# Which queue issues the first loads of a fused attention, gate and expert block, and when the biases are loaded

## The chip, the core and the metric

The kernel runs on one core of a Trainium2 chip. Its time is device microseconds of one execution. The kernel before takes 307.41 us, the median of 3 runs (307.2 to 307.61).

## The reference

The input x has 1,024 tokens (2 batches of 512) of 1,024 columns. Per batch there is a context of 1,024 rows and 1,024 columns. Cut to what matters:

```python
def fake_quant(x, scale, zp):
    q = jnp.clip(jnp.round(x / scale + zp), 0, 255)
    return (q - zp) * scale

# the "attention": a quantized product, gated by a scalar
x = x + tanh(g_xattn) * fake_quant(layernorm(x)) @ fake_quant(ctx)
# a shared MLP and two routed experts of 16, gated by a scalar
xt = layernorm(x)
z = silu(xt @ sw1 + sb1) * (xt @ sw2 + sb2) @ sw3 + sb3
y = sum over chosen experts of gate * (silu(xt @ ew1 + eb1) * (xt @ ew2 + eb2) @ ew3 + eb3)
x = x + tanh(g_ffn) * (y + z)
```

The change touches only how the first inputs come into the core. Nothing that is computed changes.

## The kernel before, in words

The tokens are eight tiles of 128 (tiles 0 to 3 are batch 0, tiles 4 to 7 batch 1). A first stage, which ends some 60 us into the run, does for each tile: statistics of the two halves (`bn`, L182, and `ag`, L186, on VectorE), the reciprocal root (`qp`, L195, on GpSimd), scale and offset (`qr`, L199 and L200), the quantized tile (`q8`, L214), the centred bf16 copy `qx` (`qc`), eight transposes on TensorE (`qt`, L225) and their copy `qT` (`qe`, L163). The context comes in eight row tiles per batch, each quantized to bytes (`c8`, L238 or L240) and centred to bf16 in `cq` (`cc`, L167 or L169). TensorE then multiplies qT by cq (`mm`, L250), and VectorE adds the product to x (`e`, L262). What follows, the second layer norm, the shared MLP, the routing, the experts and the down products, keeps TensorE at work to the end.

The order of the first stage is written out by hand. `START` (L43) is a list of steps with the engine that runs each, and the instructions of every engine stand in the order of that list; an engine does not pass an instruction that waits. `kb` steps are matmuls of zeros (L554) that fill TensorE's time. Step `pb` (L559) transposes the biases on TensorE, and `bt` (L562) copies them to where later activations take them from.

The loads are issued ahead of that list. In program order they are: the scalars `sc_in` (L118: the quantization's scales and zero points and the two gates, broadcast to 128 partitions, 3 KB); tile 0 of x in two column halves of 256 KB, by `load_x(0, 2)` (L514, which calls L133); then the list `LOADS` (L42). There `x.t` is a tile of x (512 KB, L133), `c.k` a row tile of the first context (512 KB, L508; `c.7` in two halves), `b` the biases of all hidden layers (72 rows of 512 B, L525), and `w.c.i` a weight slice of the shared MLP (512 KB in rows of 512 B, L498; in the profile sa0r, sb1r, sa1r and sb0r). Step `ld` (L594), further on in START, issues the second context and tiles 6 and 7 of x. All of these loads are issued by SyncE, so its queue alone sets their order.

Each load signals its end on a semaphore. There are eight, taken in turn, so a load that takes one again waits, on the queue that issues it, until the load eight before it has landed. By 8.9 us SyncE is at the tenth of these loads and waits in that way.

On the other engines the stage starts as follows. ScalarE loads its function table, runs a warm-up activation on a constant (L139), and takes the tanh of the gates (L528), for which it needs the scalars. VectorE sets constants, takes reciprocal, negation and a few more small results of the scalars (L145 to L153, L530, L531), and begins the statistics of tile 0. TensorE runs fillers.

Of the kernel before, what the change touches and what calls it, by code (L numbers as in the profile page):

```python
# [18 lines left out]
P = 128  # L19
# [19 lines left out]
LOWEST = -3.4028234663852886e38  # L39


LOADS = "x.1 x.3 c.0 c.1 c.2 b c.4 c.3 x.2 c.5 x.4 c.6 c.7.0 c.7.1 x.5 w.0.0 w.1.1 w.1.0 w.0.1"  # L42
START = """  # L43
bn.0.0 bn.0.1 ag.0 qa.0.dve xx.0 qp.0 kb.12 kb.1 qr.0.dve kb.3 q8.0.dve.0 qc.0.act.0 stage.0 kb.7 qt.0.0 bn.1.0 bn.1.1
bn.3.0 ag.1 bn.3.1 ag.3 qa.1.pool c8.0.0.act.0 qp.1 q8.0.dve.1 qa.3.dve qc.0.dve.1 cc.0.0.act.0 kb.2 qr.1.pool
# [32 lines left out]
def flamingo_block(  # L78
# [3 lines left out]
    nc = tc.nc  # L82
    xf = x.rearrange("b s d -> (b s) d")
# [14 lines left out]
    def slab(name, dtype, shape=(P, D)):  # L98
        return slabs.tile(list(shape), dtype, tag="slab", name=name)
# [15 lines left out]


    sc_in = const.tile([P, 6], F32, name="sc_in")
    nc.sync.dma_start(sc_in, scal.partition_broadcast(P))  # L118


    X = [None] * NT
# [5 lines left out]
    dq = [nc.sync]  # L127

    def load_x(t, parts=1):
        X[t] = slab(f"X{t}", F32)  # L130
        for h in range(parts):
            cols = ts(h, D // parts)
            dq[0].dma_start(X[t][:, cols], xf[ts(t, P), cols])  # L133


    mhalf = const.tile([P, 1], F32, name="mhalf")
# [36 lines left out]
    cols = lambda h: slice(None) if h is None else half(h)  # L173
# [337 lines left out]
    wr = {}  # L511
    NB = 2 * SC + 2 * E * EC
    br = const.tile([NB, P], F32, name="br")
    load_x(0, 2)  # L514
    for load in LOADS.split():
        kind, *at = load.split(".")
        at = [int(a) for a in at]
        if kind == "x":
            load_x(*at)
        elif kind == "c":  # L520
            load_c(0, *at)
        elif kind == "w":
            load_w(*at)
        else:
            nc.sync.dma_start(br, hbias)  # L525
# [68 lines left out]
    def ld():  # L594
        for k in range(KD):
            load_c(1, k)
        load_x(6)
        load_x(7)
# [410 lines left out]
    for n in range(SC, NC):  # L1009
        j, c = divmod(n - SC, EC)  # L1010
# [223 lines left out]
```

## Time and profile before

| | |
|---|---|
| median of 3 runs | 307.41 us |
| the profiled execution: its own time | 308.87 us |
| its span, first to last instruction | 307.1 us |
| granted TensorE clock | 0.998 |
| busy: TensorE, its weight loads | 296.7, 232.0 us |
| busy: VectorE, ScalarE, GpSimd | 216.9, 150.3, 88.0 us |
| HBM read, written | 39.76, 12.59 MB |
| chain that ended last: TensorE, DMA, SyncE's queue | 81%, 11%, 3% |

The page cuts the span in 40 slices of 7.7 us and gives a digit for the busy tenths of each. SPq is the queue of SyncE: the time in which it issues DMAs or waits to. A row of the timeline has start, duration, engine, line, operation, what it writes and reads, a count, and in brackets how long the engine stood idle before it and what ended that. A row of the stage table has the stretch, its length, busy time and count of the five engines, the granted clock, the busy share of the DMA engines and what they moved in GB/s. In the first 45 us the core reads 14.85 MB, 330 GB/s on average, nearly all of it in the queue of the hardware DMAs that SyncE issues.

### The profile page before, as it was taken

The page shows a single profiled execution, that of the slowest core. Times are in us where ns is not written, and L with a number is a line of the kernel's source. Part 1 is how long each engine was busy: PE and PEld are TensorE (multiplying, and loading weights), DVE is VectorE, ACT ScalarE, POOL GpSimd, SP SyncE. Part 2 cuts the span into 40 slices and gives each one's busy share as a digit, 9 for nine tenths or more (in the row PEclk, how much of TensorE's full clock was granted, in tenths as well). Part 3 has the DMA queues.
Part 4 walks back from the last instruction along what each step waited for, and adds up shares of the span by engine and source line. Part 5 has one row for each costly group of instructions (what it writes and reads, how often), then busy time and mean ns, then how long its engine had stood idle before and what let it go on. Part 6 is the DMA issues. An engine that isn't in the chain of part 4 may idle for free.

```text
span 307.1 us, 4234 instructions
## 1 busy us (share of the span) xinstructions
PE 296.7 (97%) x1500; PEld 232.0 (76%) x1500; DVE 216.9 (71%) x370; ACT 150.3 (49%) x213; POOL 88.0 (29%) x118
## 2 busy tenths in 40 slices
PE   8789998999999999999999999999999999999993
PEld 3344794599958888888888888888888888888883
DVE  4899988996848599864572658825489698657522
ACT  2689888777362374443251544417573548420000
POOL 2577796568422311400011110112420060000000
PEclk9999999999999999999999999999999999999999
DMA  6999960792159982540504208049999999812122
GB/s 187 413 405 310 384 235 1 237 393 89 37 148 197 216 158 41 109 170 32 174 2 116 90 2 239 34 128 356 299 334 324 339 220 298 271 74 100 77 99 75
DMA packets 39695, 56.91 MB, mean 185 GB/s; under 512 B 5531, under 2 KB 22755, under 8 KB 39666
## 3 DMA queue, kind: packets, MB, share of 16 engines
q1 hardware_dynamic: 36338, 48.16, 45.6%
q0 software_dynamic: 3328, 8.39, 14.5%
q8 instruction: 14, 0.23, 0.3%
q14 instruction: 15, 0.12, 0.1%
HBM read 39.76 MB, written 12.59 MB: 170 GB/s over the span
## 4 chain that ended last, share of the span: by engine, by line
PE 81%; DMA 11%; SPq 3%; DVE 1%; POOL 1%; issue 0%; POOLq 0%
PE pb L962 11%; DMA X<-in_dram 9%; PE sp L362 7%; PE pa L962 7%; PE pc L962 6%; PE sp L582 4%; PE b7B L406 3%; PE b6B L406 3%; PE b5B L406 3%; PE b4B L406 3%; PE b3B L406 3%; PE b2B L406 3%; PE at L250 3%; SPq L498 2%; DMA cr<-in_dram 2%; PE b7C L406 2%
## 5 line engine op out<-in xcount | busy, mean ns | idle before, releaser
L250 PE MATMUL at<-cq,qT 128*128 128x512 bf16 x128 | 29.8, 379 | 1.5 <-POOL cq L169 1.0
L250 PEld LDWEIGHTS <-qT 128*128 128x128 bf16 x128 | 12.1, 97 | 15.3 <-issue 1.9
L973 DVE SCALAR_TENSOR_TENSOR Y<-pb,tg,Y 128x512 f32<-128x512 f32 x12 | 9.0, 748 | 8.3 <-PE pb L962 8.3
L809 POOL DMA_DIRECT2D xf<-xf x8 | 7.2, 938 | 22.9 <-DMA xf<-xf 13.1
L933 POOL DMA_DIRECT2D rS<-hrouted x6 | 7.3, 1600 | 22.3 <-DMA rS<-hshared 15.2
L554 PE MATMUL pz<-zero 128*128 128x512 bf16 x43 | 12.0, 436 | 1.4 <-DVE zero L547 1.4
L973 DVE SCALAR_TENSOR_TENSOR Y<-pc,tg,Y 128x512 f32<-128x512 f32 x8 | 5.9, 749 | 10.0 <-PE pc L962 10.0
L438 POOL TENSOR_TENSOR b4s<-b4s,gates 128x512 f32<-128x512 f32 x2 | 2.6, 1279 | 34.7 <-ACT b4s L448 27.9
L262 DVE SCALAR_TENSOR_TENSOR X<-at,cx_scale,X 128x512 f32<-128x512 f32 x16 | 11.7, 745 | 0.5 <-PE at L250 0.5
L238 ACT ACTIVATE q8c<-cr,sc_in,rs 128x1024 uint8<-128x1024 f32 (+1 forms) x9 | 10.2, 1135 | 3.6 <-DMA cr<-in_dram 3.6
L182 DVE BATCH_NORM_STATS2 st<-X 128x6 f32<-128x512 f32 x16 | 10.5, 677 | 1.8 <-DMA X<-in_dram 1.8
L271 ACT ACTIVATE xn<-X,s 128x512 f32<-128x512 f32 x16 | 11.5, 718 | 0.1
L315 DVE TENSOR_TENSOR XL<-px,XH 128x512 fp32r<-128x512 f32 x16 | 10.3, 679 | 0.5 <-ACT xf L322 0.5
L167 ACT ACTIVATE cq<-q8c,nz 128x1024 bf16<-128x1024 uint8 (+1 forms) x10 | 10.4, 1056 | 0.3 <-DVE q8c L240 0.2
L554 PEld LDWEIGHTS <-zero 128*128 128x128 bf16 x43 | 4.5, 110 | 7.2 <-issue 2.7
L582 PE MATMUL sp<-XH,sb 128*128 128x256 f32 x64 | 9.6, 290 | 0.3 <-ACT XH L161 0.3
L161 ACT CAST XH<-px 128x512 fp32r<-128x512 f32 x13 | 7.2, 606 | 5.0 <-PE px L305 5.0
L656 POOL TENSOR_TENSOR xf<-XH,XL 128x1024 f32<-128x1024 f32 x4 | 9.5, 2399 | 0.0
L956 DVE TENSOR_TENSOR rB<-rB,rB 128x1024 f32<-128x1024 f32 x8 | 9.2, 1217 | 0.0
L582 PEld LDWEIGHTS sp<-XH,sb 128*128 128x128 f32 x64 | 8.2, 190 | 1.1 <-ACT XH L161 0.7
L305 PE MATMUL px<-ident,xn 128*128 128x128 f32 x64 | 8.8, 274 | 0.1
L582 PE MATMUL sp<-XH,sa 128*128 128x256 f32 x64 | 8.8, 285 | 0.0
(598 smaller groups left out, 886.5 us busy)
## 6 DMA issues: line engine op xcount, KB each, us to landing
cr<-in_dram SPq DMA_DIRECT2D x15, 512.0 KB, 8.7
x_after<-X SPq DMA_DIRECT2D x8, 512.0 KB, 6.7
xf<-xf POOLq DMA_DIRECT2D x8, 512.0 KB, 5.2
rB<-in_dram SPq DMA_DIRECT2D x8, 512.0 KB, 8.9
Y<-x_after SPq DMA_DIRECT2D x8, 512.0 KB, 8.8
out_dram<-Y SPq DMA_DIRECT2D x15, 256.0 KB, 2.2
X<-in_dram SPq DMA_DIRECT2D x7, 512.0 KB, 10.1
rS<-hrouted POOLq DMA_DIRECT2D x6, 512.0 KB, 11.6
```

The source lines that it names most:

```text
L167: nc.scalar.activation(out, q8, AF.Identity, bias=nz)
L182: nc.vector.bn_stats(st_[t][:, h, :], X[t][:, half(h)])
L250: nc.tensor.matmul(acc[t][h], qT[b][:, t % TB, k, :], cq[b][k // KH][:, k % KH, half(h)], start=(k == 0), stop=(k == KD - 1))
L262: nc.vector.scalar_tensor_tensor(xs, acc[t][h], cx_scale, xs, ALU.mult, ALU.add, accum_out=sq_[t][0][:, h : h + 1])
L271: nc.scalar.activation(xn_[t][:, half(h)], X[t][:, half(h)], AF.Square, bias=s[:, h : h + 1], scale=-float(H), accum_out=q[:, h : h + 1],)
L315: nc.vector.tensor_tensor(XL[b][q][p], px_[t, q], XH[b][q][p].bitcast(F32), ALU.subtract)
L362: nc.tensor.matmul(p, wx[:, k, :], xx[b][k // KH][:, k % KH, cols], start=first and k == 0, stop=last and k == KD - 1,)
L406: nc.tensor.matmul(p, w[:, k, :], x[:, k, :], start=f and k == 0, stop=l and k == KH - 1, skip_group_check=not first,)
L554: nc.tensor.matmul(pz[0], zero[:, :P], zero, start=True, stop=True)
L582: nc.tensor.matmul(up_[c, lo, i], w[:, k, :], x[0][k // KH][:, k % KH, lo : lo + 256], start=p == 0 and k == 0, stop=p == 2 and k == KD - 1,)
L962: nc.tensor.matmul(p, x[:, ts(t, P)], w[:, cl], start=first and k == 0 and i == 0, stop=k == KH - 1 and i == 2, skip_group_check=not first,)
L973: nc.vector.scalar_tensor_tensor(X[t][:, cl], p, tgf, X[t][:, cl], ALU.mult, ALU.add)
```

## The change: who issues the first loads

Four things are done. The scalars' load goes from SyncE's queue to ScalarE's. So does the second half of tile 0; the first half stays with SyncE, and is now its first DMA. `load_x(0, 2)` is moved up, ahead of the constants and ScalarE's table load, so that both of ScalarE's DMAs stand in front of that load in its order. And `b` moves in `LOADS` from behind `c.2` to behind `x.5`, ahead of the weight slices.

```diff
-LOADS = "x.1 x.3 c.0 c.1 c.2 b c.4 c.3 x.2 c.5 x.4 c.6 c.7.0 c.7.1 x.5 w.0.0 w.1.1 w.1.0 w.0.1"
+LOADS = "x.1 x.3 c.0 c.1 c.2 c.4 c.3 x.2 c.5 x.4 c.6 c.7.0 c.7.1 x.5 b w.0.0 w.1.1 w.1.0 w.0.1"
...
     sc_in = const.tile([P, 6], F32, name="sc_in")
-    nc.sync.dma_start(sc_in, scal.partition_broadcast(P))
+    nc.scalar.dma_start(sc_in, scal.partition_broadcast(P))
...
         for h in range(parts):
             cols = ts(h, D // parts)
-            dq[0].dma_start(X[t][:, cols], xf[ts(t, P), cols])
+            (dq[0] if h == 0 else nc.scalar).dma_start(X[t][:, cols], xf[ts(t, P), cols])
+
+
+    load_x(0, 2)
...
     br = const.tile([NB, P], F32, name="br")
-    load_x(0, 2)
     for load in LOADS.split():
```

`load_x` with one part, as all other tiles of x are loaded, issues on SyncE as before. The eight semaphores are taken in program order whoever issues, so the scalars and the two halves still take the first three. With `b` gone from its place, the loads from c.4 to x.5 each take the semaphore before the one they took; the four weight slices and all that follow take the same ones as before. On VectorE the first statistics of tile 0 move ahead of three small operations on the scalars; TensorE's and GpSimd's orders stay as they are.

## The prediction, made blind

> **What bounds the kernel now.** I read the page first (busy shares, slices, its chain), then the same chain in order of time, then a table of busy time by stage, and last the timeline of the first 54 us. In the page's slices TensorE looks full from end to end, so the question is where it is not:
>
> ```profile
> PE   8789998999999999999999999999999999999993
> DMA  6999960792159982540504208049999999812122
> ```
>
> The stage table (us of the stage, then busy us and count per engine) says it in numbers:
>
> ```profile
> 0.00:18.00 18.00, 13.96 (x65) 5.85 (x65) 12.18 (x33) 8.64 (x12) 7.94 (x18) 1.00 0.87 318
> 18.00:44.00 26.00, 25.53 (x172) 17.48 (x171) 25.31 (x57) 23.09 (x34) 20.23 (x30) 1.00 1.00 350
> 44.00:54.00 10.00, 9.21 (x64) 5.16 (x63) 7.99 (x20) 8.86 (x13) 7.43 (x13) 1.00 0.01 3
> 54.00:302.00 248.00, 248.00 (x1204) 203.48 (x1202) 170.88 (x262) 109.68 (x158) 52.37 (x58) 1.00 0.58 169
> ```
>
> From 54 to 302 TensorE has no gap; behind it lie 5.1 us of last add and store. So the time is 302.0 + 5.1, and a change can only move the point at which the unbroken part begins. TensorE idles 4.04 us before 18 (more in truth: 43 of its matmuls there, L554, are fillers on zeros), 0.47 us from 18 to 44, and 0.79 us from 44 to 54. The chain in order of time (start, us, what) shows what ends each:
>
> ```profile
> 0.87 0.39 SPq L118
> ...
> 2.25 6.61 DMA X<-in_dram
> ...
> 8.88 8.99 DMA X<-in_dram
> ...
> 17.88 3.18 SPq L498
> ...
> 33.36 11.48 DMA X<-in_dram
> ```
>
> Every link until 44.84 is a load or its issue: the DMA engines are about full (share 0.87, then 1.00), and tile 7 of x lands at 44.84 as the last big load. Two places tie TensorE to this stream, and the timeline has both:
>
> ```profile
> 3.69 0.18 DVE L145 RECIPROCAL rs<-sc_in 128x4 f32<-128x4 f32 x1 [2.38 <-DMA sc_in<-in_dram]
> 5.37 0.69 DVE L182 BATCH_NORM_STATS2 st<-X 128x6 f32<-128x512 f32 x1 [0.37 <-DMA X<-in_dram]
> 8.89 1.93 DVE L182 BATCH_NORM_STATS2 st<-X 128x6 f32<-128x512 f32 x3 [0.65 <-DMA X<-in_dram]
> 11.02 0.23 POOL L191 TENSOR_SCALAR r<-mv 128x1 f32<-128x1 f32 x1 [3.87 <-DVE mv L186]
> 16.92 0.81 PE L250 MATMUL at<-cq,qT 128*128 128x512 bf16 x3 [1.01 <-POOL cq L169]
> 24.27 0.23 PE L559 MATMUL pbt<-ident,br 72*128 72x72 f32 x1
> ```
>
> Place one: VectorE stands 0.65 us until tile 1 lands at 8.86; from its statistics GpSimd works without a pause (11.02 to 16.8) up to the piece of cq that TensorE awaits at 16.92. Place two: VectorE stands 0.78 us until 44.87 for tile 7, and the qT, sa and qx behind it on VectorE cost TensorE gaps of 0.17, 0.30 and 0.32 us before 53.37: the 0.79 us. So two paths lead to 53.4: TensorE's own, set at 16.9, which is 0.8 us ahead, and tile 7's, which decides.
>
> **The change, part by part.** *SyncE's queue.* Today it issues the scalars (0.87, 0.39 us), tile 0's halves (1.31 and 1.77, 0.42 and 0.43 us) and then tile 1, at 2.25. Afterwards the first half starts at 0.87 (0.44 earlier), and tile 1 at 0.87+0.42+0.05 = 1.34: 0.91 us earlier, as are tile 3 and the first context tiles. The biases' issue (0.75 us at 5.09) no longer stands ahead of c.4; that is worth nothing more, as the loads from 8.88 on wait for landings, not for SyncE.
>
> *What the stream gains.* From 8 us on it runs at 410 to 430 GB/s, so what matters is how much earlier it gets going. Below: 0.44 us, the shift of the first byte, if tile 1 is tied to the end of tile 0 as today. Above: 0.91, the shift of tile 1's issue. I take 0.7, about the middle, since tile 1 stands right behind the first half now but shares the engines with the second. One rule of the Trainium skill bears on this: DMA: Bandwidth & Descriptors, "Issuing engines are not separate DMA queues", says that all issuers' transfers interleave on the same 16 engines, and that a second issuer only saves the sequencer's time. By it the second ring moves no byte sooner; the sum stays with these issue times (0.44 to 0.91), and I book nothing for two rings. The rows leave some room: between 4 and 5 us, with four loads issued, the engines moved only 152 GB/s, so something other than bytes held them, and a second ring might fill that (a rival below).
>
> *Tile 0 and the scalars.* ScalarE issues the scalars at 0.88 and the half at about 1.3, instead of SyncE at 0.87 and 1.77. The scalars' landing at 3.69 frees VectorE; I keep it (between -0.1 and +0.5, since they now start side by side with the first half). In the changed program VectorE takes the first statistics three small operations earlier (at about 4.0 instead of 4.31). The second half was awaited to 5.37; issued 0.46 earlier but beside tile 1, I take 5.1, between 4.9 and 5.8. VectorE's work on tile 0, which ends at 8.24, then ends near 8.0, and 0.65 us of waiting for tile 1 covers it up to 8.9. Cost nothing, gain nothing beyond tile 1's.
>
> *ScalarE.* Two issues of about 0.43 us (SyncE's rows; ScalarE has none) push its table load (row at 0.88, 1.28 us) from 0.88 to about 1.75, so the load and the 0.20 us warm-up end at 3.25, under the 3.69 at which it waits for the scalars today. Cover left: 0.4 us; if an issue took 0.2 us more on ScalarE than on SyncE it would be used up. Here a rule speaks against the change: ScalarE: Activation LUTs, "What ACT_TABLE_LOAD costs", gives a table switch 2.66 us with its drain. From 1.75 that ends at 4.41, the tanh of the gates would come 0.9 us late, and VectorE, whose cx_scale waits for it, would delay the second statistics to some 5.2. The row shows no drain (warm-up starts at 2.17, 0.01 us after the load's end), so I book zero; by the rule it would be 0.1, again inside tile 1's wait.
>
> *The biases.* Their load moves behind x.5, whose landing is 8.7 us after its issue at 15.43, so at 24.1. No row shows a small load there: between 0 and 0.5 us after x.5, I take 0.2, as 36 KB at 415 GB/s are 0.09. TensorE's transpose of them (L559) stands in order at 24.27 and now would start at 23.6 with the stream 0.7 earlier; the biases land near 23.6. A wait of 0.1 us, at most 0.5. Queued behind it are the matmuls of tiles 0, 1 and 3 and all else on TensorE. It lies on TensorE's own path, which has the 0.8 us, so it costs nothing; without that cover it would cost itself.
>
> *The semaphores.* Each load reuses the semaphore of the load eight before, and waits for its landing. Without the biases in between, c.4 to x.5 wait for one landing earlier. The weight loads, with the biases now before them, wait for one landing later: w.0.0 for x.2 (17.87) instead of c.3 (16.66), w.1.1 for the load behind it, 1.2 us later. Their issue would be late by 1.2 minus 0.7 = 0.5 us. But w.1.1 spends 3.18 us in its issue now (17.88 to 21.06) and the same sort of load 1.45 us at 24.18: 1.7 us of it is waiting for room behind the loads ahead, and covers the 0.5. Booked at zero.
>
> **Sum.** Tile 1, tile 3 and with them GpSimd's chain and TensorE's 16.92 come 0.7 us earlier, tile 7 too (44.84 to 44.1), so 53.37 becomes 52.7: the profiled execution's 308.87 (span 307.1 and 1.77 around it) becomes 308.2. It stands 1.46 above the median of the timed runs, 307.41; I take the same 0.7 off that: 306.7, which is 0.23% less. About 0.2%, or 0.6 us, is what a measurement can tell from no change.
>
> **The rivals.**
> *The engines were the limit from the start* (tile 1 lands at 8.86 whoever issues it, as its last packets wait for their turn or for the memory). For it: tile 1 needs 6.61 us from issue to landing where a half of tile 0 needs 3.0. Against it: the 152 GB/s between 4 and 5. Gain 0 to 0.3, so 307.2. Chance 0.24.
> *Two rings fill the early hole.* The dip between 4 and 5 us (152 against the 303 GB/s of the next microsecond) is worth 0.5 us; with the 0.7 the stream comes 1.2 earlier. Tile 0's own path (about 8.0, against 8.86) then limits place one to 0.9, but TensorE's path has 0.8 in hand. 306.2. Chance 0.15.
> *The weights come too late* (the slower side). If w.0.0 and w.1.1, issued one landing later, leave the rings empty near 24 us, the whole rest of the stream slips: 1.2 us at most, against 0.7 gained, so tile 7 lands 0.5 later and the time is 307.9. It decides once the issue's slack is under 0.5 us. For it: the chain runs through those very issues (3.18, 3.04, 1.45 us). Against it: the 1.7 us of waiting for room. Chance 0.16.
> *The change does not do what it says:* the order of SyncE's queue is what the diff says, only whether ScalarE's first issue is as quick is open; that is in the first rival.
>
> **How the numbers follow.** My case has 0.45, its own range 306.4 to 307.0, and two thirds of it below 306.8. Faster by over 0.2%: 0.30 + 0.15 = 0.45. Within: 0.15 + 0.22 = 0.37. Slower: 0.18, the weights with a little of the first rival. Range: 305.9 (the second rival with 0.3 to spare) to 307.9 (half of the weights' case).
>
> **What would show it.** Tile 1's statistics on VectorE at 8.2 instead of 8.89, TensorE's matmul at 16.2, tile 7's statistics at 44.2, the last gap before 52.7, all with TensorE unbroken after. ScalarE's tanh still at 3.7. The wait at L559 under 0.5. I am wrong if tile 1 stays at 8.9, if the scalars land after 4.3, or if tile 7 comes later while tile 1 came earlier (then the weights did it).

## The result: 0.7% slower, and the profile after

| | before | after |
|---|---|---|
| median of 22 timed runs each | 308.09 us | 310.08 us |
| ratio of after to before, 95% | | 1.0069 [1.0049, 1.0089] |
| the profiled execution, its span | 308.87, 307.1 us | 310.04, 308.3 us |
| VectorE takes up the scalars, just landed | 3.69 us | 4.47 us |
| VectorE takes up the second half of tile 0, just landed | 5.37 us | 7.12 us |
| statistics of tile 1 start (VectorE) | 8.89 us | 9.91 us |
| start of TensorE's unbroken part | 53.37 us | 54.53 us |

The prediction said 306.7 us, 305.9 to 307.9. The two profiles lie 1.2 us apart, and all of it has come by 54.5 us: the start of the unbroken part moved by 54.53 - 53.37 = 1.16. The kernel before varies over its 22 runs from 306.88 to 311.06; so the parts are read from the profiles, and the whole from ratios.

The stage table of the changed kernel, in the stretches and columns of the one before:

```profile
0.00:18.00 18.00, 14.17 (x60) 5.98 (x61) 10.57 (x31) 7.57 (x11) 7.01 (x18) 0.91 0.88 331
18.00:44.00 26.00, 24.94 (x161) 15.95 (x160) 25.71 (x56) 22.41 (x32) 21.48 (x31) 1.00 0.95 341
44.00:54.00 10.00, 10.00 (x69) 6.54 (x68) 8.77 (x20) 9.59 (x14) 6.78 (x12) 1.00 0.01 2
54.00:302.00 248.00, 247.76 (x1210) 203.23 (x1208) 172.23 (x265) 110.48 (x158) 53.65 (x60) 1.00 0.58 168
```

In the first row VectorE did 10.57 us of work where it did 12.18: it is behind by 18 us. The DMA engines moved more in that row (331 GB/s against 318), so the loads as a whole are not late. In the third row TensorE has no gap left: the wait for tile 7, one of my two places, is gone, and the time is longer all the same. The granted clock is 0.91 in the first row, which is new; runs below ask whether that is the cause.

The start of the chain that ended last, in order of time (start, us, what):

```profile
1.31 5.79 DMA X<-in_dram
11.20 4.26 PE pz L556 x12
```

Before, the chain's first long load was tile 1, issued at 2.25. Now it is the second half of tile 0, issued by ScalarE at 1.31 and landed 5.79 us later, for 256 KB; and no later load is among these longest pieces. The timeline shows what waits for it (lines are 2 or 3 higher than before: L185 is the statistics, L228 the transposes, L556 the fillers, L561 the biases):

```profile
0.87 1.34 SPq L133 DMA_DIRECT2D X<-in_dram  x3
0.88 0.41 ACTq L118 DMA_DIRECT2D sc_in<-in_dram  x1
...
1.31 0.45 ACTq L133 DMA_DIRECT2D X<-in_dram  x1
...
1.80 1.28 ACT L142 ACT_TABLE_LOAD   x1 [1.80 <-PEq L1222]
...
4.47 0.18 DVE L148 RECIPROCAL rs<-sc_in 128x4 f32<-128x4 f32 x1 [3.17 <-DMA sc_in<-in_dram]
...
7.12 0.33 SPq L133 DMA_DIRECT2D X<-in_dram  x1
7.12 0.69 DVE L185 BATCH_NORM_STATS2 st<-X 128x6 f32<-128x512 f32 x1 [1.55 <-DMA X<-in_dram]
7.49 0.43 SPq L511 DMA_DIRECT2D cr<-in_dram  x1
...
8.34 0.33 SPq L133 DMA_DIRECT2D X<-in_dram  x1
...
9.91 1.87 DVE L185 BATCH_NORM_STATS2 st<-X 128x6 f32<-128x512 f32 x3
...
10.80 0.40 PE L228 MATMUL pq<-ident_b,qx 128*128 128x128 bf16 x4 [2.46 <-ACT qx L170]
...
11.04 4.42 PE L556 MATMUL pz<-zero 128*128 128x512 bf16 x12
```

The scalars land 0.8 us later than before. VectorE then stands 1.55 us until the second half is there (0.37 before), and from 7.12 it works through tile 0's small steps up to 9.91, where the row of tile 1's statistics has no bracket: VectorE did not wait for tile 1. SyncE's own rows say when tile 1 and tile 3 came. Each issue there waits for the load eight before: by that the issue at 7.12 waits for the second half, the one at 7.49 for tile 1, the one at 8.34 for tile 3. (Before, the issue at 8.88, which waited for tile 1, is the twelfth load, counted from the scalars.) So tile 1 was there by 7.49 (8.86 before) and tile 3 by 8.34 (10.12 before, by the same reckoning). The trace's own landing records put tile 1 at 6.92, ahead of the second half. The loads after tile 0 came earlier, as the change suggests, and the start of tile 1's statistics gained nothing from it, because tile 0 itself came later.

How much earlier is the stream in bytes? From stage tables of one microsecond each (GB/s):

| us | 1-2 | 2-3 | 3-4 | 4-5 | 5-6 | 6-7 | 7-8 | sum to 8, MB |
|---|---|---|---|---|---|---|---|---|
| before | 0 | 127 | 334 | 152 | 303 | 250 | 401 | 1.567 |
| after | 16 | 211 | 132 | 317 | 283 | 379 | 426 | 1.764 |

0.197 MB at the 414 GB/s that follow before are 0.5 us. Yet tile 1 came 1.9 us earlier (6.92 against 8.86) and tile 3 1.8. The rest did not come from more bytes but from a changed order: SyncE's loads overtook the second half.

### The profile page after: what moved, and what is told of

Its sections match the earlier page's. It is cut to its first block, busy times and chain, and to the rows that moved or that the text cites. A ratio compares the mean times of both kernels' runs of the same rounds, so it can differ in the third digit from the quotient of the medians.

```text
span 308.3 us, 4234 instructions
## 1 busy us (share of the span) xinstructions
PE 298.0 (97%) x1500; PEld 232.7 (75%) x1500; DVE 217.9 (71%) x370; ACT 150.1 (49%) x213; POOL 88.9 (29%) x118
## 4 chain that ended last, share of the span: by engine, by line
PE 83%; DVE 9%; POOL 3%; DMA 2%; issue 1%; ACT 0%; ACTq 0%; POOLq 0%
PE pb L964 11%; PE sp L365 7%; PE pa L964 7%; PE pc L964 6%; PE sp L584 4%; PE b7B L409 3%; PE b6B L409 3%; PE b5B L409 3%; PE b4B L409 3%; PE b3B L409 3%; PE b2B L409 3%; PE at L253 3%; DMA X<-in_dram 2%; PE pz L556 2%; DVE st L185 2%; PE b7C L409 2%
## 5 line engine op out<-in xcount | busy, mean ns | idle before, releaser
L556 PE MATMUL pz<-zero 128*128 128x512 bf16 x43 | 13.5, 476 | 1.4 <-DVE zero L549 1.4
L185 DVE BATCH_NORM_STATS2 st<-X 128x6 f32<-128x512 f32 x16 | 10.3, 672 | 1.6 <-DMA X<-in_dram 1.6
L556 PEld LDWEIGHTS <-zero 128*128 128x128 bf16 x43 | 4.8, 115 | 8.1 <-issue 4.1
L170 ACT ACTIVATE qx<-q8x,nz 128x1024 bf16<-128x1024 uint8 (+1 forms) x5 | 5.3, 1061 | 8.1 <-DVE q8x L217 5.9
```

Source lines behind the costliest of these rows:

```text
L170: nc.scalar.activation(out, q8, AF.Identity, bias=nz)
L185: nc.vector.bn_stats(st_[t][:, h, :], X[t][:, half(h)])
L556: nc.tensor.matmul(pz[0], zero[:, :P], zero, start=True, stop=True)
```

## Experiments

Each of ten kernels was timed together with the kernel before on the same chip, and a ratio compares these two. The table has what decides; "start" is that of tile 1's statistics, and the landings are those of the trace's records.

| run | scalars, first, second half landed | start | span | ratio to before, 95% |
|---|---|---|---|---|
| before | 3.7, 4.3, 5.4 | 8.89 | 307.1 | |
| after | 4.5, 4.3, 7.1 | 9.91 | 308.3 | 1.0069 [1.0049, 1.0089] |
| e1_half_first | 7.6, 4.1, 4.3 | 10.73 | 309.1 | 1.0110 [1.0053, 1.0167] |
| e2_half_only | 5.5, 6.4, 5.8 | 9.82 | 308.2 | 1.0031 [1.0014, 1.0048] |
| e3_scalars_only | 4.5, 4.3, 5.9 | 8.75 | 307.1 | 0.9994 [0.9971, 1.0016] |
| e4_biases_only | 3.7, 4.3, 5.2 | 8.98 | 305.6 | 0.9982 [0.9957, 1.0006] |
| e5_more_fillers | as after | 9.95 | 308.3 | 1.0083 [1.0056, 1.0110] |
| e6_fewer_fillers | 3.9, 4.6, 5.7 | 8.49 | 306.5 | 1.0014 [0.9993, 1.0035] |
| e7_scalars_biases | 4.5, 4.3, 5.9 | 8.68 | 307.2 | 1.0004 [0.9981, 1.0027] |
| e8_scalars_gpsimd | 8.0, 4.1, 4.3 | 11.82 | 310.6 | 1.0134 [1.0103, 1.0166] |
| e9_hold_sync | 4.1, 3.9, 4.5 | 8.14 | 306.8 | 1.0012 [0.9985, 1.0038] |
| e10_changed_again | 4.3, 4.1, 7.1 | 9.93 | 308.5 | 1.0042 [1.0016, 1.0069] |

In eleven of the twelve profiles the span less the start is 298.0 to 298.8 us (before 307.1 - 8.89 = 298.2, after 298.4), while the start itself runs from 8.14 to 11.82. Only e4_biases_only is off it, with 296.6. So in these profiles the span follows tile 1's statistics nearly one for one, and the first question is what sets their start. (Why the rest is so constant is asked under e7; it is in part luck.) A start varies by some tenths by itself: e6 issues the same loads as the kernel before, and starts at 8.49 where that starts at 8.89.

### The parts, one at a time

**e1_half_first**: the changed kernel, with the two loads of ScalarE in the other order.

```diff
-    nc.scalar.dma_start(sc_in, scal.partition_broadcast(P))
...
     load_x(0, 2)
+    nc.scalar.dma_start(sc_in, scal.partition_broadcast(P))
```

> The changed kernel with ScalarE's two loads in the other order: the half of tile 0 first, then the scalars. Theory A (order within one ring: the 128 pieces of 24 B of the scalars hold ScalarE's ring until about 4.0 us, and only then does the half move, landing at 7.10): the half now lands at 4.3 to 5.3 us, the scalars at 5 to 6.5 us; statistics of tile 0 end by about 6.5, TensorE idles under 1.5 us before its first transposes instead of 2.46, and the time falls 1 to 2 us below the changed kernel's, to within 1 us of the kernel before. Theory B (sharing: the half must take turns with the deep queue of SyncE, whichever place it has): the half still lands near 6.5 to 7, the scalars later still, and the time is that of the changed kernel or more.

The half landed early as theory A had it, but the time got worse: the scalars took the half's place. The timeline:

```profile
4.11 0.69 DVE L185 BATCH_NORM_STATS2 st<-X 128x6 f32<-128x512 f32 x1 [2.81 <-DMA X<-in_dram]
...
7.66 0.18 DVE L148 RECIPROCAL rs<-sc_in 128x4 f32<-128x4 f32 x1 [2.86 <-DMA sc_in<-in_dram]
```

3 KB issued at 1.31 landed at 7.64. So it is not the size: whichever load stands second in ScalarE's ring (its queue of DMAs) is late. The view of the DMA queues from 0 to 9 us of this run (busy tenths and GB/s in 40 slices of 0.225 us) shows what the scalars do while they pass:

```profile
DMA  0000000087699999997765343253436799999999
GB/s 0 0 0 0 0 0 0 0 100 173 237 319 364 373 382 465 446 401 256 238 183 128 128 129 92 74 147 92 128 128 219 274 437 382 455 401 473 401 382 455
...
q10 hardware_dynamic: 288, 0.27, 8.3%
```

q10 is ScalarE's ring: 128 pieces of 24 B for the scalars, 128 of 2,048 B for the half, and 32 of 4 B. From 4.5 to 6.8 us, with SyncE's loads waiting in their own ring, the engines moved only 74 to 183 GB/s. The changed kernel has its dip (132 GB/s) from 3 to 4 us, where its scalars pass; before has it (152) from 4 to 5, just after they do, so the pieces explain the dip only in part.

**e2_half_only**: the kernel before, with the second half alone on ScalarE, and `load_x(0, 2)` at its new place behind the scalars' load, which stays SyncE's first.

```diff
-            dq[0].dma_start(X[t][:, cols], xf[ts(t, P), cols])
+            (dq[0] if h == 0 else nc.scalar).dma_start(X[t][:, cols], xf[ts(t, P), cols])
...
+    load_x(0, 2)
...
-    load_x(0, 2)
```

> The kernel before with one part of the change: the second half of tile 0 issued by ScalarE; scalars first on SyncE and the biases in their old place. Theory A (the scalars ahead of the half in its ring did the harm): the half lands near 4.5 to 5.3 us (5.37 before), time within 0.7 us of the kernel before. Theory B (taking turns with SyncE's loads): the half lands at 6.3 to 7.1, TensorE idles 1.5 us or more before its first transposes, and the time is 1 to 2 us over the kernel before.

Theory A fell here in its simple form: the half, alone in its ring, landed at 5.8, between the ranges of the two theories and no earlier than in the kernel before, and now the scalars (5.5) and the first half (6.4) were late in SyncE's ring.

```profile
5.52 0.18 DVE L148 RECIPROCAL rs<-sc_in 128x4 f32<-128x4 f32 x1 [4.22 <-DMA sc_in<-in_dram]
...
6.44 1.28 DVE L185 BATCH_NORM_STATS2 st<-X 128x6 f32<-128x512 f32 x2 [0.22 <-DMA X<-in_dram]
```

Two rings delay each other's first loads. SyncE's big loads are not needed for that: by the packet records, from 2.2 to 3.8 us no data passes here but about 90 pieces of the scalars and 47 packets of the half, and the engines moved 24 GB/s from 2 to 3 us and 108 from 3 to 4. So the scalars' small pieces slow what shares with them, too. In one ring, the order is a priority: before, tile 0's three loads are all in by 5.37.

**e3_scalars_only** (the kernel before with `nc.scalar.dma_start(sc_in, ...)` as the only edit) and **e7_scalars_biases** (the same and the new `LOADS`, which is the changed kernel with only the half's move undone):

> The kernel before with one part of the change: the scalars issued by ScalarE, both halves first on SyncE. Theory A: the half is safe in SyncE's ring (lands about 4.5 to 5.0), only the scalars come late (4.2 to 4.5 us against 3.69), which is inside the wait for tile 1; no 2 us idle of TensorE, loads from tile 1 on 0.4 us earlier, time 0 to 0.8 us under the kernel before. Rival C (the scalars' late landing alone delays all of tile 0): tile 0's statistics end 0.8 us later than before and the time is 0.5 to 1 us over it.

> The changed kernel with one part undone: both halves of tile 0 are on SyncE again, first in its queue; scalars on ScalarE and the biases late, as in the change. Ring theory (what stands second in ScalarE's ring comes late, since by then the deep queue of SyncE shares the engines with it): the half lands at about 5.9 as in the run with the scalars alone, no loss of clock, time within 0.5 us of the kernel before. Rival (scalars and late biases carry part of the loss): 0.6 us or more over the kernel before.

Both are within 0.3% of the kernel before. The scalars come 0.8 us late in both and the second half at 5.9, but with the halves on one ring VectorE starts tile 1's statistics at 8.75 and 8.68, a little ahead of before. So most of the loss needs the half's move: e7 and the changed kernel differ in that and in the place of `load_x(0, 2)` in the program, and the ratios are 1.0004 against 1.0042 and 1.0069.

e7 also shows where the forecast gain went. Tile 1's statistics start 0.21 us earlier than before, and VectorE's wait of 0.78 us for tile 7 is gone, yet tile 7's statistics start at 44.8 as before (44.87). Between the two, single instructions of VectorE take longer. The first case, before and then in e7:

```profile
18.55 0.75 DVE L169 TENSOR_SCALAR cq<-q8c,nz 128x1024 bf16<-128x1024 uint8 x1
...
19.27 1.19 POOL L240 TENSOR_SCALAR q8c<-cr,rs,sc_in 128x1024 uint8<-128x1024 f32 x1 [1.30 <-PE pq L225]
```

```profile
17.70 1.62 POOL L240 TENSOR_SCALAR q8c<-cr,rs,sc_in 128x1024 uint8<-128x1024 f32 x1
...
18.29 1.57 DVE L169 TENSOR_SCALAR cq<-q8c,nz 128x1024 bf16<-128x1024 uint8 x1
```

GpSimd no longer waits before it quantizes this piece of the context, so it runs beside VectorE's instruction, and both take longer (1.62 for 1.19, 1.57 for 0.75). From 31 us on it happens again: four steps of the layer norm (L300) take 2.72 us in place of 1.92, with GpSimd's next quantization beside them, which before stood 1.44 us for its load. Some later instructions are shorter in e7 and give part of it back. The long 1.57 stands in all seven profiles in which GpSimd has begun its step and not ended it (the changed kernel, e1, e2, e3, e5, e7, e10), and 0.75 in the other five; no run tests it by itself. So the earlier stream did take away the wait for tile 7, about 0.8 us, and VectorE lost about as much beside GpSimd. That the span less the start is nearly the same before and after rests on these two being of one size. e6, e8 and e9 have neither and still lie at 298.0 to 298.8; why is not shown.

**e4_biases_only** (the kernel before with the new `LOADS` list):

> The kernel before with one part of the change: the biases' load behind x.5. Theories A and B both give no more than 0.3 us either way. Rival D (the biases arrive late for TensorE's transpose, and the weight slices wait for one landing more): a wait of 0.1 to 0.5 us at that transpose, weights issued 1.2 us later than before, and a time 0.5 to 1.5 us over the kernel before.

No loss: 0.9982, and the interval [0.9957, 1.0006] includes no change. TensorE waited 0.18 us for the biases here (before it loads them as weights, L559, at 24.21). Its profile is the one off the rule, 1.6 us better than its start would give. It has neither cost: no wait for tile 7, and the two steps of VectorE at their short 0.75 and 1.92 us, so TensorE's unbroken part begins at 51.91 in place of 53.37. Why its later loads came as they did is open, and the timed runs do not show a gain of that size.

### Is it the clock?

After the 2.46 us of idling at 10.80, the next 12 fillers took 4.42 us in place of 2.75, and the granted clock of the stage is 0.91. **e5_more_fillers** gives the changed kernel eight more fillers in front of the first transposes; **e6_fewer_fillers** takes eight from the kernel before (the second pair of lines).

```diff
-bn.0.0 bn.0.1 ag.0 qa.0.dve xx.0 qp.0 kb.12 kb.1 qr.0.dve kb.3 q8.0.dve.0 qc.0.act.0 stage.0 kb.7 qt.0.0 bn.1.0 bn.1.1
+bn.0.0 bn.0.1 ag.0 qa.0.dve xx.0 qp.0 kb.20 kb.1 qr.0.dve kb.3 q8.0.dve.0 qc.0.act.0 stage.0 kb.7 qt.0.0 bn.1.0 bn.1.1
...
-bn.0.0 bn.0.1 ag.0 qa.0.dve xx.0 qp.0 kb.12 kb.1 qr.0.dve kb.3 q8.0.dve.0 qc.0.act.0 stage.0 kb.7 qt.0.0 bn.1.0 bn.1.1
+bn.0.0 bn.0.1 ag.0 qa.0.dve xx.0 qp.0 kb.4 kb.1 qr.0.dve kb.3 q8.0.dve.0 qc.0.act.0 stage.0 kb.7 qt.0.0 bn.1.0 bn.1.1
```

> The changed kernel with eight more zero matmuls ahead of tile 0's first transposes (31 instead of 23), so that TensorE does not stand the 2.46 us after which its twelve next fillers took 4.42 instead of 2.75 us (granted clock 0.91 in the first 18 us). Clock theory (TensorE's lost clock makes the kernel slow): the twelve take 2.75 us again, granted clock back near 1.00, and the time falls 1.0 to 1.7 us. Chain theory (tile 0's late half pushes VectorE, and GpSimd behind it, 1.0 us back, and TensorE's first products wait for GpSimd anyway): the fillers are quick again, but the piece of cq comes as before, and the time falls 0 to 0.3 us.

> The kernel before with eight zero matmuls fewer ahead of tile 0's first transposes (15 instead of 23), its loads untouched: TensorE now stands about 3 us before 9.05. Clock theory: its clock falls as in the changed kernel, the next twelve fillers take about 4.4 us, and the time rises 0.8 to 1.7 us with all data on time. Chain theory: the fillers are slow too, but 1.0 us of TensorE's wait for cq at 16.9 takes most of it up, and the time rises 0.2 to 0.7 us.

The timeline has the fillers after the first transposes; first of e5:

```profile
11.08 2.75 PE L556 MATMUL pz<-zero 128*128 128x512 bf16 x12
```

and of e6:

```profile
9.39 0.61 PE L225 MATMUL pq<-ident_b,qx 128*128 128x128 bf16 x4 [2.53 <-ACT qx L167]
9.79 4.07 PE L554 MATMUL pz<-zero 128*128 128x512 bf16 x12
```

e5 has its full clock back (1.00 from 0 to 18 us) and its span is the changed kernel's, 308.3. e6 lost the clock (0.91) and shows no loss that can be told from none (1.0014 [0.9993, 1.0035]). **e10_changed_again** settles it. It is the changed kernel once more, on the chip of e9:

> The changed kernel itself, on the chip of the run with SyncE held back, so that the two stand side by side. All theories: the half lands at 7.1 us, tile 1's statistics start at 9.9, 0.4 to 0.9% over the kernel before.

In that execution TensorE idled 2.30 us, the next 12 fillers took 2.75 us, the clock did not fall (1.00 from 0 to 18 us), and the span is 308.5, no better than with the fall:

```profile
7.14 0.69 DVE L185 BATCH_NORM_STATS2 st<-X 128x6 f32<-128x512 f32 x1 [1.71 <-DMA X<-in_dram]
...
9.93 1.87 DVE L185 BATCH_NORM_STATS2 st<-X 128x6 f32<-128x512 f32 x3
...
10.82 0.40 PE L228 MATMUL pq<-ident_b,qx 128*128 128x128 bf16 x4 [2.30 <-ACT qx L170]
```

The clock is an effect of the late tile, not the cause of the time.

### What holds the second load of ScalarE's ring

**e8_scalars_gpsimd**: the changed kernel with the scalars on GpSimd's queue, so that the half is alone in ScalarE's. If the half is late because it stands behind the scalars, it should come early, and the scalars as well.

```diff
-    nc.scalar.dma_start(sc_in, scal.partition_broadcast(P))
+    nc.gpsimd.dma_start(sc_in, scal.partition_broadcast(P))
```

> The changed kernel with the scalars issued by GpSimd's queue, so that the second half of tile 0 stands first in ScalarE's ring and the first half first in SyncE's. Ring theory: both halves land at 4.0 to 4.4 us (as in the run with the half first in ScalarE's ring), tile 0's statistics end by 5.9 instead of 8.1 if the scalars land by 4.5, tile 1 lands near 7, TensorE keeps its clock, and the time is 1 to 2.5 us under the changed kernel's and 0 to 1.3 us under the kernel before. Sharing theory (a third ring slows all three): scalars or a half land at 5.5 or later, and the time is no better than the kernel before.

The half did (4.3), the scalars did not: 8.0, later than in any other run, and the time is the worst of all, 1.0134.

```profile
8.02 0.18 DVE L148 RECIPROCAL rs<-sc_in 128x4 f32<-128x4 f32 x1 [6.71 <-DMA sc_in<-in_dram]
```

A queue of its own did not protect the scalars. But GpSimd's queue is of another kind (the profile lists it as software_dynamic, the other two as hardware_dynamic): the scalars went there as 16 packets of 192 B, the first at 4.73 us, 2.5 us after their issue was over. So this run does not say that sharing made them late. For the half it says more: as the first of its ring it is early beside the same stream of SyncE, here (4.3) as in e1 (4.3); its packets are through by 3.9 us, most of them while SyncE's ring is still at the first half. As the second it meets tile 1 and what follows. **e9_hold_sync** removes these loads for as long as tile 0 is under way. SyncE first stores one element of the second half to a scratch word, for which it has to wait until the half has landed, and issues tile 1 only then.

```diff
+    seen = spill.tile([1, 1], F32, name="seen")
+    with tc.manual_schedule():
+        nc.sync.dma_start(seen, X[0][0:1, D - 1 : D])
+        for load in LOADS.split():
...
```

> The changed kernel with SyncE held back: after the first half of tile 0 it issues a store of one element of the second half to a scratch word (4 bytes, read by nothing; this is the added work), for which it waits until that half has landed, and only then tile 1 and the rest. So ScalarE's two loads share the engines with the first half alone. Sharing theory (the half lands at 7.1 because tile 1 and the contexts, issued by SyncE from 1.3 us on, take turns with it): the half now lands at 4.8 to 5.6 us, tile 0's statistics end near 6.3 instead of 8.06, tile 1 is issued at about 5.2 and lands at 8.3 to 9.3, TensorE keeps its clock, and the time is 0.7 to 2 us under the changed kernel's, near that of the kernel before. Rival (a second load in ScalarE's ring is slow by itself): the half lands at 6.5 or later, tile 1 some 3 us behind it, and the time is 1 us or more over the changed kernel's.

```profile
1.31 0.45 ACTq L133 DMA_DIRECT2D X<-in_dram  x1
...
4.11 0.18 DVE L148 RECIPROCAL rs<-sc_in 128x4 f32<-128x4 f32 x1 [2.81 <-DMA sc_in<-in_dram]
...
4.51 0.30 SPq L519 DMA_DIRECT2D seen<-X  x1
...
4.86 0.84 SPq L133 DMA_DIRECT2D X<-in_dram  x2
...
5.13 0.68 DVE L185 BATCH_NORM_STATS2 st<-X 128x6 f32<-128x512 f32 x1
...
8.14 2.00 DVE L185 BATCH_NORM_STATS2 st<-X 128x6 f32<-128x512 f32 x3
```

Same issue at 1.31, same place behind the scalars in the same ring: it lands at 4.50 in place of 7.12, and the scalars at 4.1. On the same chip the median is 308.83 us, against 310.21 for e10_changed_again and 308.58 for the kernel before. With tile 1 issued 3.5 us later than in the changed kernel, 1.4 us of loss is gone. That is the cause of the half's lateness, shown from both sides: it comes with the sharing (e10) and goes with it (e9), with ring, order and issue times of tile 0's three loads kept. The time goes with it; e9 holds the whole stream back as well, so its time alone does not say how much is the half's, but e7, where only the half's move is undone, comes to the same (1.0004).

The trace's packet records fit it. In the changed kernel ScalarE's ring moves the 24 B pieces of the scalars from 2.1 to 3.9 us, and the half's 128 packets of 2,048 B only from 4.2 to 6.6, in turns with 129 packets of 4,096 B from SyncE's ring, which had been given six loads by then. In e9 the pieces pass from 2.2 to 3.6 and the half's packets from 2.8 to 4.1. So of the 2.6 us about 1.4 are a later start behind the scalars, and the rest the turns.

No version that ran clearly beats the kernel before. e4_biases_only is the nearest.

## Why the prediction was wrong, step by step

*SyncE's queue* held: first half at 0.87, the row of three issues there (first half, tile 1, tile 3) is as worked out.

*What the stream gains* held for the bytes and not for tile 1. In bytes it is 0.5 us ahead by 8 us, at the low end of my 0.44 to 0.91. Tile 1 gained 1.9 and tile 3 1.8, more than even the rival of two rings (1.2), since they passed the second half.

***Tile 0 and the scalars* is the step that failed.** I had the second half at 5.1, bounded by 4.9 and 5.8; it landed at 7.10, 1.3 us over the bound. I had the scalars at 3.69, at most 4.2; they were there at 4.47, past the 4.3 that I had named as a sign of being wrong. I took the durations from rows in which one ring served these loads in order, added a little for company, and did not ask whose turn it is when two rings hold work. And the step "covered by 0.65 us of waiting for tile 1" was wrong twice. That cover was tile 1's lateness, which the same change was meant to take away: with tile 1 there at 6.92 it is gone, whatever the half does. Then tile 0's own work becomes the bound: from the second half's statistics (7.12) VectorE needs 2.79 us to reach tile 1's, so 9.91. With the half at 5.1 that would have been 7.9; I had this limit (about 8.0) in the second rival, but with the half on time.

*The sum* most likely would not have come out even with the half on time. The nearest runs are e3 and e7, with the half at 5.9, 0.1 over my bound: they start 0.1 and 0.2 earlier, VectorE no longer waits for tile 7, and no gain shows in their times: 0.9994 [0.9971, 1.0016] and 1.0004 [0.9981, 1.0027], where my 0.23% would be 0.9977, inside the first interval and outside the second. I took a load that comes earlier as work that ends earlier by as much. What I put at nothing is that GpSimd's work on the context comes earlier with it and then runs beside VectorE's (0.75 us becomes 1.57, 1.92 becomes 2.72). e9 has what I forecast for place one, tile 1's statistics at 8.14, but with a stream held back, and its time shows no gain either (1.0012 [0.9985, 1.0038]).

*TensorE's 0.8 us in hand* was no cover either. GpSimd's first step after tile 1's statistics slipped from 11.02 to 11.98, and the end of the gaps by 1.16. The stage table of before had the hint: VectorE is busy 25.31 of 26 us from 18 to 44 (25.71 now), so a late VectorE has little room to catch up. That this is how the delay is carried to 54 us is read from the rows; no run here tests it by itself.

*ScalarE* held: two issues of 0.41 and 0.45 us, table load at 1.80 (1.75 forecast), warm-up over by 3.29, well before the scalars. The rule on table loads with a drain (the Trainium skill, ScalarE: Activation LUTs, "What ACT_TABLE_LOAD costs": 2.66 us for a switch) would have put the end of the load at 4.46; it ended at 3.08.

*The biases* held: L561 starts at 25.45 without a wait, and e4 shows no loss. *The semaphores and the weights* held: the rival in which weights come too late asks for a wait behind tile 7, and from 44 to 54 us TensorE is never idle. So my slower side rested on the wrong mechanism: that it allowed for a loss at all was luck, and its 0.18 was too small.

*The rule on issuing engines* (the Trainium skill, DMA: Bandwidth & Descriptors, "Issuing engines are not separate DMA queues") was right: all issuers' transfers interleave on the same engines (128 packets of the half among 129 of SyncE's), and the bytes gained what the earlier issue gave. I read it as "a second ring brings nothing" and booked no cost. Its word "interleave" is the cost: what stood in front of the deep queue now shares with it.

What stays open: why the scalars' pieces hold a ring for 1.3 us (e9) to 3.4 us (e1), why two engines side by side take longer, why e4's later loads came earlier in its profile, and the size of the loss between 0.4% (e10), 0.7% (22 runs) and 0.8% (e5).

## What to carry to other kernels

A queue's order is a priority. Moving an urgent load to a second queue saves the issue time (0.4 to 0.9 us here) and gives up that priority: the deep queue that it left now takes turns with it, and what stands second in the new one comes late (7.1 us against 5.4). As the first of the new queue the half came early in e1 and e8 (4.3), with the scalars late instead (7.6 and 8.0), and not even so in e2 (5.8), beside the scalars' small pieces. Before a wait is booked as cover, ask whether the change itself removes that wait; and when loads come earlier, ask which engine then works beside which.

## What the runs showed of the hardware that was not expected

A broadcast of 3 KB to 128 partitions in pieces of 24 B landed 2.8 us after the start of its issue as the first load of the only ring (0.87 to 3.67), and 6.3 us after (1.31 to 7.64) as the second of its ring; while it passed there, the engines moved some 120 GB/s where 400 came before and after.

An instruction of VectorE (`cq`, 128x1024) took 0.75 us in five profiles and 1.57 in the seven in which GpSimd was already at a quantization of 128x1024 (e7: 17.70 to 19.32) when it began.

The granted TensorE clock fell after idling of 2.46, 2.53 (e2 and e6), 3.01 and 4.74 us (the 12 fillers then took 4.07 to 5.18 us) and not after 0.85, 1.61 and 2.30 (2.75 us). The Trainium skill (TensorE: Matmul & The Clock Gate, "Part 1: The HAM clock gate") has the clock fall after an idle window of about 3.4 us; here it fell after 2.46 us of idling, and the measurement decides. The length of the gap is not all of it: in the changed kernel the clock was still 1.00 from 10.8 us, when TensorE resumed, to 11.9, and 0.50 from 12.0 to 15.3.
